# A graph layer on one core: two pieces of the edge list sorted side by side, and the order of the cold passes that follows from it

## The chip, the cores and the metric

The kernel runs on one core of a Trainium2 chip. The metric is device time in microseconds: before the change the median of three runs is 2072.53 us (2072.35 to 2072.87). The profile is one further execution of its own.

## The reference: what is computed

A layer over 6250 nodes of 256 features and 200000 edges, all in float32. The edges are sorted by `dst`, which is skewed towards low nodes; `src` is random.

```
xn = layernorm(x)
w  = sigmoid(relu(xn[dst] @ W1 + b1) @ W2 + b2)          # one weight per edge's far node
num, den = segment_sum(xn[dst] * w, src), segment_sum(w, src)
x  = x + where(den > 0, num / max(den, 1e-12), 0) + mix(xn)
x  = x + experts(layernorm(x))                          # 6 experts, the best 2 of them weighted
```

The part that matters here is the segment sum: for each of 200000 edges a row of the far node is added to the near node `src`. Six experts of three 256x256 layers are computed for every node.

## The kernel before, in words

**Rows.** Node by node a row `y = (xn * w, w)` is written to DRAM as three bfloat16 terms of 258 (`y_rows`, 774 values a row), by `node_rows`.

**Edges in pieces.** The kernel sorts the edges by `src` itself, in pieces of 65536 edges (128 partitions by 512). Two pieces are cold: `a` (edges 65536 on) and `c` (131072 on). The first 65536 edges are the hot piece `b`, whose `dst` are few: its edges are counted into small matrices instead of gathered. The last 3392 edges ("few", 27 tiles of 128) are gathered and scattered into a DRAM table one tile at a time (`few_edges`: a gather L519, a matmul L535, a copy `sm` by ACT, a scatter L540).

**The sort** (`sort`, L349) is a bitonic merge sort. Keys are made on DVE (`keys_of`), rows of 512 are sorted (`rows_sorted`, 9 levels), then seven levels merge over partitions (`merged`): turn the piece by four 128x128 transposes on PE and one copy by ACT (`turned`, L313 and L314), min/max steps, turn back, nine more min/max steps over the row. A step is two DVE instructions over 256 elements (L277 min, L278 max); the first step of a level negates one side (L262) and is two or four instructions. Each piece has its own tiles (`k_a`, `t_a` and so on) and its own chain of steps. When it is done, the sorted list is written to DRAM (L355).

**Order.** The order on each engine is written by hand: parts of the work are generators (`Line`), and `run` takes from a list of lines the first one that is due on a model clock; each step tells how much engine time it takes (`took` for a sort step) and how long its line then waits (`TURN` after a turn). First come a's sort, the node rows and the few edges' comparisons, with the sorts of c and b as filler behind them; `line_a2` is c's sort and `line_b` b's, and c stands ahead of b in the lists. Then the cold steps begin, one each 2200 ns of the model clock while the few edges last and one each 1300 ns after that, with the sorts, the head statistics (`head_squares`, `heads`) and a check for equal keys (`equal_keys`, which reads b's list back) between them.

**Cold steps** (`Cold`). For a block of two node tiles and a piece, the window of the sorted list that can hold its edges (12 tiles of 128 for each node tile) is loaded from DRAM by SP (L794), turned on PE (L818), copied by ACT (L820) and decoded on DVE (L827, L829, L868). Then for each tile of 128 edges: POOL gathers the rows of y by an indirect DMA (L880), DVE makes a one-hot matrix (L888), PE multiplies and sums (L905, three matmuls). Gathers are issued 10 steps ahead of the matmul (`AHEAD`), into 20 buffers (`GBUF`). `passes` (L836) lists what is done in which order: the first `LEAD` = 4 blocks take piece a alone, then the same 4 blocks take c alone, and from then on each block takes both. Sums of a alone are held as parts; there are `HELD` = 17 buffers for parts and sums. A window of c can be loaded only when c is sorted (`piece_sorted`, L919, which otherwise runs c's sort to its end on the spot).

**Main loop** (`Work`, L1349 on). Each cold step is followed by other work worth its share: node terms (L1102), hot sums of a block (one-hots L1049 and L1051, matmuls L1058 and L1077), and the experts (L1230, L1247). The hot sums of a block wait until the block's cold sums exist; the experts of a group of two blocks wait for its hot sums. The share leaves some 150 us (by the model) for the end.

The weights' loads on ACT's queue (L946 to L954) stand in the order behind the few edges; they go into memory that the few edges' tiles used.

Of the kernel before, what the change touches and what calls it, by code (L numbers as in the profile page):

```python
# [17 lines left out]
P = 128  # L18
# [6 lines left out]
LOW = 13  # L25
# [1 line left out]
HB = 8  # L27
GBUF = 20
AHEAD = 10
HELD = 17  # L30
LEAD = 4
LAST = 150000.0


# [15 lines left out]
def kernel(  # L50
# [45 lines left out]
    nc = tc.nc  # L96
# [64 lines left out]
    lists = {p.name: dram.tile([p.n + p.cap * P], FP, name=f"list_{p.name}") for p in pieces}  # L161
# [40 lines left out]
    sq_ps = sps.__enter__()  # L202
# [15 lines left out]
    def pool_of(p):  # L218
        return sp_small

    cnts = const.tile([P, len(pieces), NTHR], FP, name="cnts")
    raw = {}

    def raw_load(p):
        ends = []
        for nm, ap in (("src", src), ("dst", dst)):
            t = pool_of(p).tile([P, p.row], I32, name=f"{nm}_{p.name}")
# [6 lines left out]
    def keys_of(p):  # L234
        s_i, d_i = raw[p.name]
        pool = pool_of(p)
        key = pool.tile([P, p.row], I32, name=f"t_{p.name}", bufs=2)
        if p is hot:

            low = pool.tile([P, p.row], I32, name=f"k_{p.name}", bufs=2)  # L240
            nc.vector.tensor_scalar(low, s_i, BN - 1, None, op0=ALU.bitwise_and)
            nc.vector.scalar_tensor_tensor(low, d_i, 8, low, op0=ALU.logical_shift_left, op1=ALU.bitwise_or)
            nc.vector.tensor_scalar(key, s_i, 8, 18, op0=ALU.logical_shift_right, op1=ALU.logical_shift_left)
            nc.vector.tensor_tensor(key, key, low, op=ALU.bitwise_or)
        else:
            nc.vector.scalar_tensor_tensor(key, s_i, LOW, d_i, op0=ALU.logical_shift_left, op1=ALU.bitwise_or)
        k = pool.tile([P, p.row], FP, name=f"k_{p.name}", bufs=2)
# [32 lines left out]


    def took(n):
        return 2 * max(90.0, 60.0 + 1.05 * n)

    def rows_sorted(p, k):

        h = 1
        while h < p.row:
            g = h
            while g:  # L290
                o = pool_of(p).tile([P, p.row], FP, name=f"k_{p.name}", bufs=2)
                if g == h:
                    first(k, o, h, last=2 * h == p.row)
                else:
                    step(k, o, g)
                k, g = o, g // 2
                yield took(p.row // 2), 0
            h *= 2
        return k

    def turned(p, k, name, back):

        o = pool_of(p).tile([P, max(p.row, P)], FP, name=f"{name}_{p.name}", bufs=2)
        if p.row < P:
            ps = sq_ps.tile([P, 4 * P], FP, name="turn")
            a, b = (p.row, P) if back else (P, p.row)
            nc.tensor.transpose(ps[:b, :a], k[:a, :b], ident[:a, :a])
            nc.scalar.copy(o[:b, :a], ps[:b, :a])
            return o[:b, :a]
        for c0 in range(0, p.row, 4 * P):  # L310
# [3 lines left out]
            nc.scalar.copy(o[:, c0 : c0 + 4 * P], ps)  # L314
        return o

    def merged(p, k, m):

        t = turned(p, k, "t", False)
        yield 0, TURN  # L320
        g = h = 1 << (m - 1)
        while g:
            o = pool_of(p).tile([P, max(p.row, P)], FP, name=f"t_{p.name}", bufs=2)
            if p.row < P:
                o = o[: p.row, :P]
# [5 lines left out]
            yield took(p.row // 2 if p.row >= P else P // 2), 0  # L331
        k = turned(p, t, "k", True)
        yield 0, TURN
        g = p.row // 2
        while g:
            o = pool_of(p).tile([P, max(p.row, P)], FP, name=f"k_{p.name}", bufs=2)
            o = o[:, : p.row]
            step(k, o, g)
            k, g = o, g // 2
            yield took(p.row // 2), 0  # L340
        return k

    TURN = 2300.0


    pad = sp_small.tile([P, max(p.cap for p in pieces)], FP, name="pad")
    nc.vector.memset(pad.bitcast(I32), BASE | ((1 << LOW) - 1) << LOW)

    def sort(p):  # L349
        k = keys_of(p)  # L350
        yield 3.0 * p.row, 0
        k = yield from rows_sorted(p, k)
        for m in range(1, 8):
            k = yield from merged(p, k, m)
        nc.sync.dma_start(lists[p.name][: p.n].rearrange("(p t) -> p t", p=P), k)  # L355
        nc.sync.dma_start(lists[p.name][p.n :].rearrange("(p t) -> p t", p=P), pad[:, : p.cap])

    def counts(i):


        p = pieces[i]
        junk = pool_of(p).tile([P, p.row], BF, name=f"junk_{p.name}")
# [412 lines left out]
    with tc.manual_schedule(engines=ORDERED):  # L775
        clock[0] = 6000.0
        line_d.due = 12000.0
        line_l.due = 16000.0
        line_u[1].before = line_u[2].before = lines_y
        line_t.before = [line_l]  # L780
        line_u[0].due = 9000.0
        first_lines = [line_u[0], line_l, line_d] + lines_y + [line_a, line_t]
        while any(a.open for a in first_lines):
            run(first_lines + [line_q, line_h, line_u[1], line_a2, line_u[2], line_b], clock[0] + 1000.0)
        starts_of(0)


# [140 lines left out]
    known = [cold[0]]  # L928
    with tc.manual_schedule(engines=ORDERED):
        cold_edges = Cold(lambda p: p is cold[0] or piece_sorted(p))  # L930
        beside = [line_c, line_u[1], line_q, line_h, line_a2, line_u[2], line_b, line_e]
# [54 lines left out]


    line_w = Line(expert_loads())
    beside = [line_w, line_u[1], line_q, line_h, line_a2, line_u[2], line_b, line_e]
# [508 lines left out]
```

## Time and profile before

| what | us |
|---|---|
| median of three runs | 2072.53 |
| the profiled execution, its own time | 2076.93 |
| its span in the trace | 2075.1 |
| PE busy (85%) | 1761.2 |
| DVE busy (62%) | 1278.1 |
| POOL busy (58%), of it 1176 cold gathers 1133.0 | 1208.6 |
| ACT busy (28%) | 580.7 |
| first cold gather issued | 249.7 |
| lists written: a, c, b | 229.7, 420.8, 549.0 |
| first expert matmul (L1230) | 662.6 |
| last cold gather, last cold matmul | 1867.6, 1872.8 |

The page of the profile names engines by short names: PE is the matmul engine and PEld its weight load, DVE the vector engine, ACT the scalar engine, POOL the engine that issues the gathers, SP the one that issues most other DMAs. A row of the page's groups gives line, engine, operation, result and operands, how often, busy time and the mean in ns of one, and after the bar how long its engine had been idle and for whom. In a timeline a line begins with start and duration in us, and ends with the idle time before it and who ended that. In the table by stages each engine's busy time is followed by its count of instructions in brackets, and the row ends with the granted clock of PE, the share of the DMA engines and GB/s.

### The profile page before, as it was taken

What the parts mean: (1) busy time and instruction counts of PE and PEld (TensorE: products, weight loads), DVE (VectorE), ACT (ScalarE), POOL (GpSimd) and SP (SyncE); (2) the same over time, 40 slices, a digit from 0 to 9 for tenths busy, and PEclk for the clock granted to TensorE, in tenths of its full rate; (3) what the DMA queues carried; (4) which work ended last, traced back from release to release, by engine and by line L of the source; (5) the groups of instructions that cost most, each with busy time, mean ns of one, the idle gap of its engine ahead of it and who ended that gap; (6) DMA issues with size and microseconds to landing.
All of it is one profiled execution on the core that took longest, in us unless ns stands there. A gap on an engine that the chain in (4) does not pass through costs nothing.

```text
span 2075.1 us, 30397 instructions
## 1 busy us (share of the span) xinstructions
PE 1761.2 (85%) x9539; PEld 1175.5 (57%) x9539; DVE 1278.1 (62%) x5292; ACT 580.7 (28%) x1197; POOL 1208.6 (58%) x1243
## 2 busy tenths in 40 slices
PE   0564389635588999999999999999999999999997
PEld 0343277524355666666666666665666756566555
DVE  8799867948786555566565455555546565464322
ACT  6864464100011212222121221212212122222332
POOL 0000167877646777777777777777777777770000
PEclk9775589856689999999999999999999999999999
DMA  9562267567646566676666666666666566661000
GB/s 254 175 207 89 59 153 174 122 166 239 181 111 169 163 166 193 163 196 161 194 162 163 196 164 195 163 160 194 165 194 164 158 195 164 196 161 27 1 10 14
DMA packets 163586, 320.56 MB, mean 154 GB/s; under 512 B 31353, under 2 KB 104298, under 8 KB 163418
## 3 DMA queue, kind: packets, MB, share of 16 engines
q0 software_dynamic: 80800, 241.85, 44.1%
q1 hardware_dynamic: 77262, 76.15, 11.8%
q10 hardware_dynamic: 5356, 0.55, 0.3%
q8 instruction: 77, 1.26, 0.3%
q14 instruction: 91, 0.75, 0.1%
HBM read 285.06 MB, written 33.39 MB: 153 GB/s over the span
## 4 chain that ended last, share of the span: by engine, by line
PE 62%; DVE 8%; DMA 6%; issue 2%; POOL 1%; ACT 1%; SPq 0%; ACTq 0%; DVEq 0%; POOLq 0%
PE px L1230 23%; PE pu L905 15%; PE px L1247 11%; DMA gt<-y_rows,dsts 5%; PE ph L1077 5%; PE ph L1058 4%; DVE fr L1051 1%; PE px L1217 1%; DVE to L1049 1%; PE px L1137 1%; PE ph L1102 1%; DVE k_b L277 1%; DVE k_b L278 1%; POOL gt L880 1%; DVE hot L888 1%
## 5 line engine op out<-in xcount | busy, mean ns | idle before, releaser
L880 POOL DMA_INDIRECT gt<-y_rows,dsts x1176 | 1133.0, 963 | 634.9 <-DVE srcs L829 247.5
L905 PE MATMUL pu<-gt,hot 128*128 128x258 bf16 x3528 | 593.2, 285 | 28.6 <-DMA gt<-y_rows,dsts 27.4
L905 PEld LDWEIGHTS <-hot 128*128 128x128 bf16 x3528 | 355.4, 102 | 370.3 <-issue 292.8
L1239 ACT ACTIVATE h<-px,eb_t 128x512 f32<-128x512 f32 (+1 forms) x312 | 206.5, 662 | 477.4 <-PE px L1230 476.5
L1230 PE MATMUL px<-fT,ew_t 128*128 128x512 f32 (+1 forms) x624 | 303.9, 583 | 0.0
L1230 PE MATMUL px<-h,ew_t 128*128 128x512 f32 (+1 forms) x624 | 296.1, 569 | 0.0
L1247 PE MATMUL px<-ew_t,h 128*128 128x256 f32 (+1 forms) x1176 | 295.3, 379 | 0.0
L888 DVE TENSOR_SCALAR hot<-count,loc 128x128 bf16<-128x128 bf16 x1176 | 271.1, 271 | 20.6 <-PE pu L905 20.1
L1256 DVE SCALAR_TENSOR_TENSOR acc<-px,gate,acc 128x256 f32<-128x256 f32 (+1 forms) x294 | 128.7, 478 | 219.4 <-PE px L1247 219.0
L1051 DVE TENSOR_SCALAR fr<-count,rdl 128x128 bf16<-128x128 bf16 x884 | 226.6, 271 | 40.7 <-PE ph L1058 40.1
L1247 PEld LDWEIGHTS px<-ew_t,h 128*128 128x128 f32 (+1 forms) x1176 | 204.0, 190 | 25.8 <-issue 4.8
L1058 PE MATMUL ph<-to,fr 128*128 128x256 bf16 x884 | 183.7, 284 | 21.0 <-DVE fr L1051 15.6
L1049 DVE TENSOR_SCALAR to<-count,hloc 128x256 bf16<-128x256 bf16 x612 | 183.7, 302 | 7.4 <-PE ph L1058 7.2
L1060 ACT CAST cn<-ph 128x256 bf16<-128x256 f32 x150 | 54.5, 372 | 299.0 <-PE ph L1058 298.4
L1077 PE MATMUL ph<-yh,cn 128*128 128x258 bf16 x882 | 129.3, 274 | 0.8 <-ACT cn L1060 0.7
L1058 PEld LDWEIGHTS <-fr 128*128 128x128 bf16 x884 | 87.7, 99 | 63.8 <-DVE fr L1051 42.1
L1087 DVE TENSOR_TENSOR cs<-ph,cs 128x258 f32<-128x258 f32 x49 | 20.9, 427 | 152.4 <-PE ph L1077 151.2
L1230 PEld LDWEIGHTS px<-fT,ew_t 128*128 128x128 f32 x624 | 98.4, 195 | 23.4 <-issue 16.5
L1230 PEld LDWEIGHTS px<-h,ew_t 128*128 128x128 f32 x624 | 96.0, 190 | 22.6 <-issue 18.2
L1077 PEld LDWEIGHTS <-cn 128*128 128x128 bf16 x882 | 86.0, 98 | 18.4 <-issue 5.2
L563 PE MATMUL turn<-ident,xs 128*128 128x128 f32 (+1 forms) x98 | 27.5, 402 | 78.1 <-ACT xs L554 73.1
L563 PEld LDWEIGHTS turn<-ident,xs 128*128 128x128 f32 (+1 forms) x98 | 16.9, 194 | 88.4 <-issue 50.1
(242 smaller groups left out, 1767.1 us busy)
## 6 DMA issues: line engine op xcount, KB each, us to landing
gt<-y_rows,dsts POOLq DMA_INDIRECT x1176
xs<-in_x_dram SPq DMA_DIRECT2D x24, 512.0 KB
y_rows<-ys SPq DMA_DIRECT2D x10, 774.0 KB
table<-zero SPq DMA_DIRECT2D x50, 129.0 KB
tb<-table SPq DMA_DIRECT2D x49, 129.0 KB
xnT_d<-xnT SPq DMA_DIRECT2D x12, 512.0 KB
xt<-xnT_d SPq DMA_DIRECT2D x12, 512.0 KB
u<-in_x_dram SPq DMA_DIRECT2D x12, 512.0 KB
```

The lines of the kernel that those rows point to most:

```text
L880: nc.gpsimd.indirect_dma_start(out=gt.rearrange("p k w -> p (k w)"), out_offset=None, in_=y_rows, in_offset=bass.IndirectOffsetOnAxis(ap=d ...
L888: nc.vector.tensor_scalar(hot1, count[:, half * P : (half + 1) * P], loc[:, j : j + 1], None, op0=ALU.is_equal)
L905: nc.tensor.matmul(self.pu, hot1, gt[:, k], start=(start and k == 0), stop=(stop and k == TERMS - 1))
L1049: nc.vector.tensor_scalar(made[j1], count, loc[:, j1 : j1 + 1], None, op0=ALU.is_equal)
L1051: nc.vector.tensor_scalar(fr, count[:, :P], rdl[:, d1, j1 : j1 + 1], None, op0=ALU.is_equal)
L1058: nc.tensor.matmul(pa, matrices[i], made[j], start=(j == j0), stop=(j == j1 - 1))
L1060: nc.scalar.copy(cn[:, d], pa)
L1077: nc.tensor.matmul(pu[:, :W], cn[:, d, s * P : (s + 1) * P], yh[:, d, k], start=(d == 0 and k == 0), stop=(d == HOT - 1 and k == TERMS - 1),)
L1230: nc.tensor.matmul(ph[:, :rows], w[:, e, c, f * P : (f + 1) * P], ins[:, c, :rows], start=(c == 0), stop=(c == CB - 1),)
L1239: nc.scalar.activation(h[:, f, :rows], ph[:, :rows], AF.Relu, bias=bc)
L1247: nc.tensor.matmul(po[:r, j - j0], h2[:, c, j * P : j * P + r], ew_t[2][:, e, c, :], start=(c == 0), stop=(c == CB - 1),)
L1256: nc.vector.scalar_tensor_tensor(acc[:r, j, :], po[:r, j - j0], gate[:r, j, e : e + 1], acc[:r, j, :], op0=ALU.mult, op1=ALU.add)
```

## The change

Pieces c and b are sorted by one chain: their keys stand in the two halves of tiles of 1024 (`k_cb`, `t_cb`), each min/max instruction covers 512 elements instead of 256 (the first steps 256 instead of 128), a turn is eight transposes and two copies, and both lists are written when the one sort ends. There is one line for it, `line_b`, in the place of `line_a2` and `line_b`; a is sorted as before. `LEAD` is 6 instead of 4, so six blocks (144 gathers) take a alone, then the same six take c alone. `HELD` is 18. The model's price of a sort step is 150 + 1.05 n ns an instruction instead of 60 + 1.05 n (at least 90). The pace of the cold steps no longer slips when a step overruns it (`due += 2200.0` for `due = max(due + 2200.0, clock[0])`, and so for 1300). c's counts and starts are asked for by `piece_sorted(cold[1])` at the latest when both lines are through.

```diff
-HELD = 17
-LEAD = 4
+HELD = 18
+LEAD = 6
...
+    ROW = 512
+    def keys_of(ps, name):
+        key = sp_small.tile([P, len(ps) * ROW], I32, name=f"t_{name}", bufs=2)
+        for i, p in enumerate(ps):
+            s_i, d_i = raw[p.name]
+            part = key[:, i * ROW : (i + 1) * ROW]
...
     def took(n):
-        return 2 * max(90.0, 60.0 + 1.05 * n)
+        return 2 * (TT0 + 1.05 * n)
-    def rows_sorted(p, k):
+    def rows_sorted(k, name, width):
         h = 1
-        while h < p.row:
+        while h < ROW:
...
-                o = pool_of(p).tile([P, p.row], FP, name=f"k_{p.name}", bufs=2)
+                o = sp_small.tile([P, width], FP, name=f"k_{name}", bufs=2)
...
-                yield took(p.row // 2), 0
+                yield took(width // 2), 0
...
+    TT0 = 150.0
...
-    def sort(p):
-        k = keys_of(p)
-        yield 3.0 * p.row, 0
-        k = yield from rows_sorted(p, k)
+    def sort(ps):
+        name, width = "".join(p.name for p in ps), len(ps) * ROW
+        k = keys_of(ps, name)
+        yield 3.0 * width, 0
+        k = yield from rows_sorted(k, name, width)
         for m in range(1, 8):
-            k = yield from merged(p, k, m)
-        nc.sync.dma_start(lists[p.name][: p.n].rearrange("(p t) -> p t", p=P), k)
-        nc.sync.dma_start(lists[p.name][p.n :].rearrange("(p t) -> p t", p=P), pad[:, : p.cap])
+            k = yield from merged(k, name, width, m)
+        for i, p in enumerate(ps):
+            nc.sync.dma_start(lists[p.name][: p.n].rearrange("(p t) -> p t", p=P), k[:, i * ROW : (i + 1) * ROW])
+            nc.sync.dma_start(lists[p.name][p.n :].rearrange("(p t) -> p t", p=P), pad[:, : p.cap])
...
-    line_a, line_a2, line_b = (Line(sort(p)) for p in pieces)
+    line_a, line_b = Line(sort(pieces[:1])), Line(sort(pieces[1:]))
...
-        while line_a2.open or line_u[1].open:
-            run([line_u[1], line_a2], clock[0] + 1000.0)
+        while line_b.open or line_u[1].open:
+            run([line_u[1], line_b], clock[0] + 1000.0)
...
-            due = max(due + 2200.0, clock[0])
+            due += 2200.0
...
-            due = max(due + 1300.0, clock[0])
+            due += 1300.0
             run(beside, due)
+        piece_sorted(cold[1])
```

More of the change, by code (lines that the diff above doesn't have):

```diff
@@ L216 @@
     nc.vector.tensor_scalar(odd, even, SIGN, None, op0=ALU.bitwise_xor)
-    def pool_of(p):
-        return sp_small
     cnts = const.tile([P, len(pieces), NTHR], FP, name="cnts")
@@ L226, in raw_load @@
         for nm, ap in (("src", src), ("dst", dst)):
-            t = pool_of(p).tile([P, p.row], I32, name=f"{nm}_{p.name}")
+            t = sp_small.tile([P, p.row], I32, name=f"{nm}_{p.name}")
             nc.sync.dma_start(t, ap[p.start : p.start + p.n].rearrange("(p t) -> p t", p=P))
@@ L232 @@
     raw_load(cold[0])
[L234 to L247, printed above, removed]
+    ROW = 512
[4 more added lines that the diff above has]
+            part = key[:, i * ROW : (i + 1) * ROW]
+            if p is hot:
+                low = sp_small.tile([P, len(ps) * ROW], I32, name=f"k_{name}", bufs=2)[:, :ROW]
+                nc.vector.tensor_scalar(low, s_i, BN - 1, None, op0=ALU.bitwise_and)
+                nc.vector.scalar_tensor_tensor(low, d_i, 8, low, op0=ALU.logical_shift_left, op1=ALU.bitwise_or)
+                nc.vector.tensor_scalar(part, s_i, 8, 18, op0=ALU.logical_shift_right, op1=ALU.logical_shift_left)
+                nc.vector.tensor_tensor(part, part, low, op=ALU.bitwise_or)
+            else:
+                nc.vector.scalar_tensor_tensor(part, s_i, LOW, d_i, op0=ALU.logical_shift_left, op1=ALU.bitwise_or)
+        k = sp_small.tile([P, len(ps) * ROW], FP, name=f"k_{name}", bufs=2)
         ki = k.bitcast(I32).rearrange("p (t two) -> p t two", two=2)
@@ L282, in took @@
     def took(n):
-        return 2 * max(90.0, 60.0 + 1.05 * n)
-    def rows_sorted(p, k):
+        return 2 * (TT0 + 1.05 * n)
+    def rows_sorted(k, name, width):
         h = 1
-        while h < p.row:
+        while h < ROW:
             g = h
             while g:
-                o = pool_of(p).tile([P, p.row], FP, name=f"k_{p.name}", bufs=2)
+                o = sp_small.tile([P, width], FP, name=f"k_{name}", bufs=2)
                 if g == h:
-                    first(k, o, h, last=2 * h == p.row)
+                    first(k, o, h, last=2 * h == ROW)
                 else:
@@ L296, in rows_sorted, with turned @@
                 k, g = o, g // 2
-                yield took(p.row // 2), 0
+                yield took(width // 2), 0
             h *= 2
         return k
[L301 to L310, printed above, removed]
+    def turned(k, name, width):
+        o = sp_small.tile([P, width], FP, name=name, bufs=2)
+        for c0 in range(0, width, 4 * P):
             ps = sq_ps.tile([P, 4 * P], FP, name="turn")
@@ L315, in turned, with merged @@
         return o
-    def merged(p, k, m):
-        t = turned(p, k, "t", False)
+    def merged(k, name, width, m):
+        t = turned(k, f"t_{name}", width)
         yield 0, TURN
@@ L322, in merged @@
         while g:
-            o = pool_of(p).tile([P, max(p.row, P)], FP, name=f"t_{p.name}", bufs=2)
-            if p.row < P:
-                o = o[: p.row, :P]
+            o = sp_small.tile([P, width], FP, name=f"t_{name}", bufs=2)
             if g == h:
@@ L330, in merged @@
             t, g = o, g // 2
-            yield took(p.row // 2 if p.row >= P else P // 2), 0
-        k = turned(p, t, "k", True)
+            yield took(width // 2), 0
+        k = turned(t, f"k_{name}", width)
         yield 0, TURN
-        g = p.row // 2
+        g = ROW // 2
         while g:
-            o = pool_of(p).tile([P, max(p.row, P)], FP, name=f"k_{p.name}", bufs=2)
-            o = o[:, : p.row]
+            o = sp_small.tile([P, width], FP, name=f"k_{name}", bufs=2)
             step(k, o, g)
             k, g = o, g // 2
-            yield took(p.row // 2), 0
+            yield took(width // 2), 0
         return k
+    TT0 = 150.0
     TURN = 2300.0
@@ L347 @@
     nc.vector.memset(pad.bitcast(I32), BASE | ((1 << LOW) - 1) << LOW)
-    def sort(p):
-        k = keys_of(p)
-        yield 3.0 * p.row, 0
-        k = yield from rows_sorted(p, k)
+    def sort(ps):
[3 more added lines that the diff above has]
+        k = yield from rows_sorted(k, name, width)
         for m in range(1, 8):
-            k = yield from merged(p, k, m)
-        nc.sync.dma_start(lists[p.name][: p.n].rearrange("(p t) -> p t", p=P), k)
-        nc.sync.dma_start(lists[p.name][p.n :].rearrange("(p t) -> p t", p=P), pad[:, : p.cap])
+            k = yield from merged(k, name, width, m)
+        for i, p in enumerate(ps):
+            nc.sync.dma_start(lists[p.name][: p.n].rearrange("(p t) -> p t", p=P), k[:, i * ROW : (i + 1) * ROW])
+            nc.sync.dma_start(lists[p.name][p.n :].rearrange("(p t) -> p t", p=P), pad[:, : p.cap])
     def counts(i):
         p = pieces[i]
-        junk = pool_of(p).tile([P, p.row], BF, name=f"junk_{p.name}")
+        junk = sp_small.tile([P, p.row], BF, name=f"junk_{p.name}")
         for b in range(SB - 1 if p is hot else 0, NTHR, SB if p is hot else 1):
@@ L783 @@
         while any(a.open for a in first_lines):
-            run(first_lines + [line_q, line_h, line_u[1], line_a2, line_u[2], line_b], clock[0] + 1000.0)
+            run(first_lines + [line_q, line_h, line_u[1], line_u[2], line_b], clock[0] + 1000.0)
         starts_of(0)
@@ L930 @@
         cold_edges = Cold(lambda p: p is cold[0] or piece_sorted(p))
-        beside = [line_c, line_u[1], line_q, line_h, line_a2, line_u[2], line_b, line_e]
+        beside = [line_c, line_u[1], line_q, line_h, line_u[2], line_b, line_e]
         run(beside[1:], clock[0] + 9000.0)
@@ L988 @@
     line_w = Line(expert_loads())
-    beside = [line_w, line_u[1], line_q, line_h, line_a2, line_u[2], line_b, line_e]
+    beside = [line_w, line_u[1], line_q, line_h, line_u[2], line_b, line_e]
     with tc.manual_schedule(engines=ORDERED):
```

## The prediction

> **What bounds the kernel now.** I read the slices of the page first, then busy time by stages, then the timeline of POOL, and last the timeline of DVE and ACT around the sort.
>
> ```profile
> PE   0564389635588999999999999999999999999997
> DVE  8799867948786555566565455555546565464322
> POOL 0000167877646777777777777777777777770000
> PEclk9775589856689999999999999999999999999999
> ```
>
> Each digit is a fortieth of the span (52 us). PE is full only from slice 13 on; before that it has idle time and a low granted clock. POOL starts at 250 us, stands at 7 (never 9), dips at slice 11 and stops at 1868.
>
> ```profile
> 0.00:249.50 249.50, 102.30 (x362) 65.85 (x363) 215.10 (x674) 152.72 (x327) 1.62 (x12) 0.72 0.53 158
> 249.50:454.00 204.50, 148.22 (x983) 119.33 (x981) 155.13 (x500) 73.49 (x187) 155.43 (x135) 0.81 0.62 146
> 454.00:549.00 95.00, 53.33 (x273) 38.09 (x273) 72.97 (x251) 8.70 (x18) 73.18 (x74) 0.65 0.72 212
> 549.00:662.50 113.50, 82.41 (x489) 51.40 (x490) 85.00 (x430) 14.38 (x39) 64.27 (x67) 0.80 0.52 144
> 662.50:1873.10 1210.60, 1188.23 (x6703) 783.52 (x6701) 688.05 (x3216) 271.74 (x518) 914.06 (x957) 0.99 0.64 175
> 1873.10:2075.10 202.00, 186.72 (x736) 117.35 (x734) 61.87 (x226) 59.68 (x110) 0.00 (x0) 0.96 0.04 11
> ```
>
> Busy PE, PEld, DVE, ACT, POOL with counts. I cut at events: first gather (249.5), last scatter of the few edges (454), end of the last sort (549), first expert matmul L1230 (662.5), last cold matmul L905 (1873.1). What limits the middle is seen one gather at a time:
>
> ```profile
> 1210.97 0.95 POOL L880 DMA_INDIRECT gt<-y_rows,dsts  x1 [0.30 <-issue]
> 1212.23 0.96 POOL L880 DMA_INDIRECT gt<-y_rows,dsts  x1 [0.30 <-issue]
> 1213.49 0.95 POOL L880 DMA_INDIRECT gt<-y_rows,dsts  x1 [0.30 <-issue]
> ```
>
> 0.95 us plus a fixed 0.30: POOL is saturated although the slices say 7. From 662.5 to 1867.6 it issues 957 gathers, 1.26 us each, and after 664 never waits longer than 0.31. At 662.5 it has issued 81 + 72 + 67 = 220 and PE has used 200, the whole 20 buffers of lead; the lead drains, and PE idles 22 us in that stage (21 of them after 1100). So **POOL's row of 1176 gathers bounds the kernel**, PE almost as tight; the end is last gather + 5.5 + 202. POOL loses time in one place: 549 to 662.5, 67 gathers where 90 fit.
>
> The sort ends late for a reason that is not DVE:
>
> ```profile
> 453.99 1.49 POOL L540 DMA_INDIRECT table<-sm,few_row  x1 [0.30 <-issue]
> 457.51 0.42 ACTq L946 DMA_DIRECT2D rw_t<-in_L_ffn_router_w_dram  x1
> 459.17 0.59 ACT L314 COPY t_b<-turn 128x512 f32<-128x512 f32 x1 [28.04 <-DMA eb_t<-in_L_ffn_expert_b_dram]
> 459.79 0.90 DVE L262 SCALAR_TENSOR_TENSOR t_b<-t_b 128x128 f32<-128x128 f32 x4 [20.71 <-ACT t_b L314]
> ```
>
> (POOL, ACT and DVE of one timeline.) The weight loads on ACT's queue reuse memory that the last scatter still reads; ACT is held 28 us, the sort's copy stands behind them, DVE idles 20.7. POOL sets this moment.
>
> **The change, part by part.** Counts and places come from the order of both programs' instructions.
>
> *Price of a step.* Rows of DVE:
>
> ```profile
> L277 DVE TENSOR_TENSOR k_b<-k_b 128x256 f32<-128x256 f32 x99 | 41.6, 421 | 12.1 <-ACT k_b L314 10.8
> L262 DVE SCALAR_TENSOR_TENSOR k_c<-k_c 128x256 f32<-128x256 f32 x2 | 0.8, 422 | 0.0
> L760 DVE TENSOR_TENSOR xt<-xt 128x512 f32<-128x512 f32 x1 | 0.7, 691 | 7.7 <-DMA wt_a<-list_c 7.7
> 432.63 0.25 DVE L888 TENSOR_SCALAR hot<-count,loc 128x128 bf16<-128x128 bf16 x1
> 432.80 0.42 DVE L277 TENSOR_TENSOR k_b<-k_b 128x256 f32<-128x256 f32 x1
> 433.13 0.42 DVE L278 TENSOR_TENSOR k_b<-k_b 128x256 f32<-128x256 f32 x1
> 433.58 0.42 DVE L277 TENSOR_TENSOR k_b<-k_b 128x256 f32<-128x256 f32 x1
> ```
>
> A min/max pair starts every 0.78 us (0.39 a step, they overlap), a one-hot takes 0.17. Doubling the width adds 691 - 421 = 0.27: a joint step is 0.66, a pair 1.32 where two pairs were 1.56. A joint first step is about 0.36 (four of 128x128 take 0.90). Bounds for the joint pair: 1.1 (each 0.27 + 0.27, overlap hiding all the rest) to 1.56 (no saving). I take 1.32, from the nearest row. Over 120 pairs the sort sheds some 30 us of DVE; the question is what waits for it.
>
> *To the first gather.* Ahead of the end of a's sort stood 63 steps of c (3 for keys 1.4, 28 firsts 6.3, 32 steps 12.5: 20 us); now 45 joint ones (7 for keys 4.2, 20 firsts 7.2, 18 steps 11.9: 23), and the few edges' last comparison comes before it (1 us). DVE is 215 of 249 busy here, so it is paid: 249.7 becomes 253.2 (bounds 247 to 257). After a: 34 steps (13 us) against 20 (13 us).
>
> *To the last scatter.* POOL's order has 74 cold gathers ahead of scatter 27, not 81: 7 x 1.255 = 8.8 less. DVE sheds about 36 us here (322 steps become 140), all beside POOL. 253.2 + 204.3 - 8.8 = **448.7**. POOL's only stalls (scatters waiting 3.7, 3.0, 2.0 for ACT) are kept.
>
> *To the end of the joint sort.* DVE resumed 5.8 after the scatter; a turn now has eight transposes and a second ACT copy, +0.59: 455.1. Left then are 94 steps (before: 172): 8 firsts 2.9, 43 pairs 56.8, 50 one-hots 8.3, decodes 2.0, and five turns. A turn left DVE idle some 1.2; four more transposes (1.1) and fewer one-hots in the gap make it 2.7: 13.5. Sum 83.5, **538.6** where c and hot ended at 420 and 549.
>
> *POOL runs dry.* This is new. No gather of c can come before 538.6, so a alone feeds POOL: six blocks, 144 gathers. The last 32 sort steps are forced in one go ahead of one-hot 123, when a's last pass asks for c's first window. With 20 buffers POOL gets to gather 133 at 448.7 + 1.8 + 59 x 1.27 = 525.4; PE comes free of the last turn 18 steps (12 us) before the end, 526.6; ten more gathers last to 539.3. Number 144 stands behind c's window: list written (549.02 to 552.78 before, 3.8), two window loads (0.9 + 1.9), transpose, copy, decode: 8 us, so POOL resumes at **546.6** with 143 issued, 7 us lost. Before had 152 by then.
>
> *To the first expert matmul.* Hot sums need c's parts now: block 0 only at cold matmul 168, then one block every 24 (30.2 us). A block's burst took 14.3 us (563.26 to 577.55), so DVE (14 + 24 x 0.17 + 6 of sums) has room, and POOL's lead of up to 20 gathers rides over it: the loss of 23 gathers goes. But the first L1230 stands at cold 248, not 200: 546.6 + 97 x 1.26 + 3.5 = 672.3 for cold 240, a burst and 3 more: **689.5**, 27 later.
>
> *To the end.* PE's order from there holds the same work but 48 gathers' matmuls less (976 to 928; 0.50 each, 24 us): 1188 - 24 = 1164 busy. POOL: 256 issued, 920 x 1.26 + 5.5 = 1165. Both equal; I add 5 for their catching on each other: 1170, where 1210.6 were. The tail is identical in both orders: 202. Four more DVE adds L913 (0.42) and two more decodes hide under POOL; at 2 us in all if not. HELD adds one buffer of 18, never the limit here.
>
> Sum: 689.5 + 1170 + 202 = 2061.5 against the span 2075.1, **13.6 less**. The profiled execution took 2076.93, the median is 2072.53, 2.6 below the span; so **2059**.
>
> **Rivals.**
> - *POOL starves longer; slower.* Every microsecond by which c's first window comes after 546.6 is paid in full: break-even at 560. It comes so if the wide step saves nothing (43 x 0.24 = 10) and turns expose all their transposes (another 10): +20, **2079**. For it: POOL has nothing else to issue. Against: 691 ns is measured.
> - *PE can't fill the last stage.* If its 22 us of idle stay, 1164 + 22: 2077.5, **2075**. For: 1164 against 1165 leaves no slack. Against: those idles came after the lead was used up.
> - *POOL's first stage tightens too; more gain.* To the last scatter I kept 195.5 us, but POOL's own work there is 101 x 1.255 + 27 x 1.98 = 180. If DVE's lighter load ends the stalls and the long gathers (15) and the first gather stays at 249.7 (3.5), all that follows moves up by 19: **2040**. For it: 36 us of DVE gone from that stage. Against: those stalls come at its start, from scatters that wait for ACT.
> - *Wider steps slow POOL.* Gathers take 1.03 us beside the sort (83.11 us for 81) and 0.955 later. If a gather waits for the step it meets, the extra 0.07 grows by 691/421 to 0.12: 190 POOL operations x 0.046 = 9, **2068**. The Trainium skill, GPSIMD Engine Reference, section 1 Specifications, says that POOL's SBUF interfaces are shared with VectorE and that instructions with two SBUF inputs contend; the slower gathers agree. It speaks against the change only by length, since the wide steps are fewer.
>
> **How the numbers follow.** Forecast 0.52, starving 0.18, PE 0.14, tight first stage 0.10, slower POOL 0.06. A difference under 0.2% (4 us) can't be told here from none. Faster: 0.50 + 0.10 + 0.03 = 0.63; same: 0.02 + 0.11 + 0.02 = 0.15; slower: 0.18 + 0.03 + 0.01 = 0.22. The range runs from the tight first stage to the starving case, 2040 to 2080.
>
> **What would show it.** First gather near 253, last scatter near 449, joint steps of 690 ns, list_c written near 539, a gap in POOL around gather 144 ending near 547 and no gaps of over 1 us from there to 690, first expert matmul near 690, last cold matmul near 1860, 202 after. It is wrong if list_c is written after 552, or if POOL waits for buffers again between 547 and 690, or if PE idles over 15 us after that.

## The result, and the profile after

The changed kernel takes 2066.50 us, the median of 7 runs (2062.76 to 2070.45), against 2072.18 us for the kernel before in 7 runs on the same chip (2068.03 to 2072.87): a ratio of 0.9974, 95% interval 0.9962 to 0.9987. It is faster, by 5.7 us, where 13.6 were forecast. On two of the four chips used further below every kernel takes some 14% longer, so for the experiments ratios to the kernel before on the same chip are compared, and not times. Line numbers have shifted a little: the cold gather is L877 now (L880 before), the cold matmul L902 (L905), min and max L278 and L279 (L277 and L278), a turn's copy L309 (L314), the first expert matmul L1228 (L1230), the list's write L352 (L355).

The slices of the page after:

```profile
PE   0474279746468899999999999999999999999997
DVE  8689966657657765565646555564655666464322
POOL 0000077877777777777777777777777777760000
PEclk9666579956678999999999999999999999999999
```

POOL's dip (the 4 in the twelfth slice before) is gone: it stands at 7 or 8 from its first full slice on. But its fifth slice is empty, where a 1 stood, and DVE has 6 and 8 in its second and third slices where it had 7 and 9: something in the first 250 us became slower. Three rows of the busy times by stages, cut at the same events as before (up to the first gather; from the joint list to the first expert matmul; from there to the last cold matmul):

```profile
0.00:263.20 263.20, 102.41 (x362) 62.69 (x363) 216.34 (x643) 158.89 (x351) 1.62 (x12) 0.70 0.50 150
...
541.40:699.30 157.90, 117.16 (x709) 74.82 (x710) 100.60 (x514) 15.44 (x44) 119.51 (x127) 0.80 0.67 186
699.30:1861.60 1162.30, 1159.23 (x6557) 767.32 (x6556) 685.40 (x3173) 270.42 (x513) 871.63 (x916) 1.00 0.64 176
```

The first stage is 13.7 us longer than before (263.2 to 249.5). In the third row PE is busy 1159.2 of 1162.3 us: it idles 3.1 us where it idled 22. POOL's last gather is at 1848.7 and the last cold matmul at 1861.4, 12.7 us behind, where it was 5.2. So PE, and no longer POOL, looks like the bound of this stage; a run below shows it for the kernel with six blocks alone, by taking work off PE.

| event, us | before | forecast | after |
|---|---|---|---|
| a's list issued | 229.7 | | 245.0 |
| first gather | 249.7 | 253.2 | 263.3 |
| last scatter of the few edges | 454.0 | 448.7 | 455.7 |
| joint list issued (before: c, b) | 420.8, 549.0 | 538.6 | 541.4 |
| gather 144 | | 546.6 | 551.85 |
| first expert matmul | 662.6 | 689.5 | 699.3 |
| last cold matmul | 1872.8 | 1859.5 | 1861.4 |
| end of the span | 2075.1 | 2061.5 | 2063.8 |
| the execution's own time | 2076.93 | | 2065.69 |

POOL around the end of the joint sort:

```profile
540.53 1.02 POOL L877 DMA_INDIRECT gt<-y_rows,dsts  x1 [0.30 <-issue]
541.86 0.94 POOL L877 DMA_INDIRECT gt<-y_rows,dsts  x1 [0.30 <-issue]
...
550.60 0.95 POOL L877 DMA_INDIRECT gt<-y_rows,dsts  x1 [0.30 <-DVE hot L885]
551.85 0.95 POOL L877 DMA_INDIRECT gt<-y_rows,dsts  x1 [0.30 <-PE pu L902]
```

No gap: the dry spell that was forecast for 539.3 to 546.6 did not come. The joint sort's steps (a row of the groups) and ACT's copy that it resumes with after the last scatter (issued at 455.69):

```profile
L278 DVE TENSOR_TENSOR k_cb<-k_cb 128x512 f32<-128x512 f32 x99 | 67.4, 680 | 13.8 <-ACT k_cb L309 13.0
```
```profile
460.85 1.07 ACT L309 COPY t_cb<-turn 128x512 f32<-128x512 f32 x2 [17.77 <-DMA eb_t<-in_L_ffn_expert_b_dram]
```

A joint step takes 680 ns where 691 was assumed, and a pair starts every 1.32 to 1.33 us (1.32 assumed). The hold of ACT behind the last scatter is there as before: ACT has waited 17.8 us, and the copy starts 5.2 us after the scatter.

What delays the first gather is seen in ACT's first turn of a, in whom DVE waits for up to the issue of a's list, and in the sums of busy time up to there. The kernel before (the turn, DVE's waits up to 229 us: us in total, times, longest; the sum up to 229.6):

```profile
95.35 0.56 ACT L314 COPY t_a<-turn 128x512 f32<-128x512 f32 x1
```
```profile
DVE yh L600 <- ACT w L586: 9.1, 1, 9.1
DVE ys L600 <- ACT w L586: 2.4, 2, 1.4
DVE k_a L277 <- ACT k_a L314: 0.9, 1, 0.9
```
```profile
sum 229.60, PE 90.42 PEld 58.73 DVE 201.47 ACT 141.78 POOL 1.62; mean PE 18.08 PEld 11.75 DVE 40.30 ACT 28.36 POOL 0.32
```

The kernel after (the waits up to 244 us, the sum up to 244.7):

```profile
113.93 0.59 ACT L309 COPY t_a<-turn 128x512 f32<-128x512 f32 x1 [2.03 <-PE turn L308]
```
```profile
DVE yh L597 <- ACT w L583: 10.3, 1, 10.3
DVE ys L597 <- ACT w L583: 6.0, 4, 3.6
DVE t_a L263 <- ACT t_a L309: 5.1, 3, 2.7
DVE yh L605 <- ACT yh L603: 2.8, 1, 2.8
```
```profile
sum 244.70, PE 90.69 PEld 55.72 DVE 205.17 ACT 149.10 POOL 1.62; mean PE 18.14 PEld 11.14 DVE 41.03 ACT 29.82 POOL 0.32
```

The first turn of a, with which the seven merge levels start, is 18.6 us later. In the order of DVE's instructions 171 others stand ahead of the first step behind that turn, not 162, with 4 joint steps more. The nine more are instructions of the node rows (L595 to L605), which have come in front of a's steps. Some of them wait for ACT, and a's chain waits behind them. Up to the end of a's sort DVE is busy 205.2 us (before 201.5) and idle 39.5 (before 28.1). So 3.7 us of the delay are more work and 11.4 are idle time. By all rows of the two lists of waits, some 7 us of the idle time are waits of the node rows for ACT (20.5 us, before 13.8), and some 5 are waits of a's sort for its own turns (5.8 us, before 0.9).

**Theory.** The model's new price of a sort step (`TT0`) makes `run` take a's steps less densely in the first stage; the late first gather that follows is paid to the end, and hides the joint sort's end. The gain comes from six blocks, which close POOL's lull. **Rivals**: the joint steps put in front of a's sort delay it; or an earlier first gather would only open the dry spell; or it is the joint sort that gains.

### The profile page after: what moved, and what is told of

It reads as the page before. It is cut to its first block, busy times and chain, and to the rows that moved or that the text cites. A ratio compares the mean times of both kernels' runs of the same rounds, so it can differ in the third digit from the quotient of the medians.

```text
span 2063.8 us, 30158 instructions
## 1 busy us (share of the span) xinstructions
PE 1756.6 (85%) x9541; PEld 1171.1 (57%) x9541; DVE 1256.2 (61%) x5000; ACT 577.4 (28%) x1199; POOL 1213.7 (59%) x1243
## 4 chain that ended last, share of the span: by engine, by line
PE 68%; DVE 4%; DMA 3%; issue 1%; ACT 1%; POOL 0%; SPq 0%; DVEq 0%; POOLq 0%; ACTq 0%
PE px L1228 25%; PE pu L902 16%; PE px L1245 12%; PE ph L1075 5%; PE ph L1056 4%; DMA gt<-y_rows,dsts 3%; PE px L1215 1%; PE px L1135 1%; PE ph L1100 1%; DVE to L1047 1%; DVE fr L1049 1%; PE px L1128 0%; PE px L1141 0%; PE pT L815 0%; PE turn L308 0%
## 5 line engine op out<-in xcount | busy, mean ns | idle before, releaser
L877 POOL DMA_INDIRECT gt<-y_rows,dsts x1176 | 1136.3, 966 | 618.9 <-DVE srcs L826 261.1
L902 PE MATMUL pu<-gt,hot 128*128 128x258 bf16 x3528 | 598.8, 285 | 48.1 <-DMA gt<-y_rows,dsts 38.3
L902 PEld LDWEIGHTS <-hot 128*128 128x128 bf16 x3528 | 354.7, 102 | 395.7 <-issue 305.6
L1228 PE MATMUL px<-fT,ew_t 128*128 128x512 f32 (+1 forms) x624 | 301.4, 578 | 0.0
L1228 PE MATMUL px<-h,ew_t 128*128 128x512 f32 (+1 forms) x624 | 296.3, 569 | 0.0
L1228 PEld LDWEIGHTS px<-fT,ew_t 128*128 128x128 f32 x624 | 97.2, 193 | 23.3 <-issue 16.6
L1228 PEld LDWEIGHTS px<-h,ew_t 128*128 128x128 f32 x624 | 95.9, 190 | 22.9 <-issue 18.5
L817 ACT COPY keys<-pT 128x25 f32<-128x25 f32 (+2 forms) x56 | 10.5, 187 | 251.3 <-PE pT L815 250.0
```

What stands on the lines that cost most here:

```text
L877: nc.gpsimd.indirect_dma_start(out=gt.rearrange("p k w -> p (k w)"), out_offset=None, in_=y_rows, in_offset=bass.IndirectOffsetOnAxis(ap=d ...
L902: nc.tensor.matmul(self.pu, hot1, gt[:, k], start=(start and k == 0), stop=(stop and k == TERMS - 1))
L1228: nc.tensor.matmul(ph[:, :rows], w[:, e, c, f * P : (f + 1) * P], ins[:, c, :rows], start=(c == 0), stop=(c == CB - 1),)
```

## The experiments

The experiments are four groups of four kernels, each group on a chip of its own. Only ratios to the kernel before are compared between groups; each group ran that kernel too. It took 2348.14 and 2371.90 us on the chips of the first two groups and 2076.48 and 2074.08 us on those of the last two.

### The price of a step: old price in the changed kernel

```diff
     def took(n):
-        return 2 * (TT0 + 1.05 * n)
+        return 2 * max(90.0, 60.0 + 1.05 * n)
```

> The changed kernel with the model's old price of a sort step (at least 90, 60 + 1.05 n ns an instruction), all else as changed. In the order of DVE the same 45 joint steps stand ahead of the end of a's sort, but 162 other instructions ahead of a's first turn in place of 171. Theory A, the new price spread a's steps so that DVE waits for ACT in the first stage, and the 13.6 us by which the first gather came later are paid at the end: first gather 250 to 254, time 2054 to 2058. Rival B, the wide joint steps in front of a's sort delay it: first gather 260 or later, time 2064 to 2068. Rival C, an earlier first gather only opens the gap ahead of gather 144 that the prediction spoke of: first gather 252, a gap of some 8 us in POOL near 545, time 2061 to 2065.

Ratio 0.9949 (0.9925 to 0.9973) on a slower chip, first gather 252.3. Again, with the changed kernel beside it on the other slower chip:

> The changed kernel once more, unaltered, so that the experiments have it beside them on their own chip and there is a second trace of it. On the first chip it was 0.9974 of the kernel before, with its first gather at 263.3 us and the list of the joint sort issued at 541.4. If the late first gather lies in the order that the planner chose, it is again between 262 and 267, and the ratio to before 0.995 to 1.000. If the 263.3 was a chance of one execution (the profile before had 249.7), the first gather comes near 253. On a chip with a lower granted clock PE is the bound of the last stage in both kernels; then the gain of POOL's shorter row counts less and the ratio is 0.998 to 1.004.

> The changed kernel with the planner's old price of a sort step, once more, now with the changed kernel beside it on the same chip. If the new price is what puts the first gather at 263, and that delay is paid at the end, this one is 8 to 12 us (0.4 to 0.5%) faster than the changed kernel, with its first gather at 250 to 254. If POOL or PE takes the delay up again before the end, the two are within 0.2% of each other, although the first gathers differ by 11 us.

The changed kernel 1.0024 (0.9999 to 1.0049), first gather 267.6; with the old price 0.9961 (0.9937 to 0.9985), first gather 254.5. The ratios lie 0.0063 apart, some 15 us, more than the 8 to 12 expected. And on a chip as fast as that of the result:

> The changed kernel a third time, as the bar for the two beside it. First gather between 262 and 269. Ratio to before 0.995 to 0.999 on a chip whose PE is granted its full clock in the last stage (0.9974 on the first), 1.000 to 1.005 on a slow one (1.0024 on the second).

> The changed kernel with the old price of a sort step once more. On slow chips it was 0.995 and 0.996 of before, 0.0064 below the changed kernel. If the delay of the first gather is paid whole on a chip with the full clock too, the ratio is 0.990 to 0.993, 10 to 13 us below the changed kernel. The rival: there PE is full in the last stage (3.1 us idle in the trace after), an earlier POOL only meets a full PE, and less than half of it, under 6 us, is left: 0.9945 to 0.9975.

The changed kernel 0.9962 (0.9949 to 0.9975), first gather 263.6; with the old price **0.9904** (0.9888 to 0.9919), first gather 254.2: 13.2 us of median for 9.4 us of first gather in the two traces. The rival that a full PE swallows the earlier start is refuted. With the old price ACT's first turn of a is at 98.05, where it is 113.93 in after and 95.35 in before. The spans of these two traces differ by 18.2 us: 9.4 from the first gather, 3.9 from the last stage (1162.6 and 1166.5), 3.3 from the tail (199.0 and 202.3), 1.6 from the rest; the first is the order's, the others vary between executions too.

### The price alone in the kernel before, and the joint steps in front of a

The price edit in the kernel before, which has no joint step:

```diff
-        return 2 * max(90.0, 60.0 + 1.05 * n)
+        return 2 * (150.0 + 1.05 * n)
```

> The kernel before with the new price of a sort step alone (150 + 1.05 n ns), pieces sorted one after the other and four blocks of a. Theory A: first gather 258 to 264 in place of 249.7, though no step is wide; the cold steps then stand denser beside the sort (first expert matmul at cold step 216, not 200), which wins some of it back: time 2068 to 2078. Rival B: first gather 247 to 253, time 2062 to 2070.

Ratio 1.0072 (1.0044 to 1.0099), more than the 0.3% at most that was expected; first gather 264.4, with the first turn as late as after:

```profile
116.18 0.59 ACT L314 COPY t_a<-turn 128x512 f32<-128x512 f32 x1 [1.69 <-PE turn L313]
```

The changed kernel without the joint sort as filler in the first lines, which leaves 23 joint steps ahead of the first decode where there were 65:

```diff
-            run(first_lines + [line_q, line_h, line_u[1], line_u[2], line_b], clock[0] + 1000.0)
+            run(first_lines + [line_q, line_h, line_u[1], line_u[2]], clock[0] + 1000.0)
```

> The changed kernel with the joint sort left out of the lines that run beside a's sort: 23 joint steps stand ahead of the first decode in place of 65, so some 27 us of DVE work move behind the first gather. Theory A (order by price) and B (wide steps in the way) both expect the first gather 15 to 27 us earlier, 236 to 248. They part at the end: by B the whole kernel follows, 2050 to 2058. By A together with the dry spell of the prediction the joint sort ends no earlier, near 545, POOL has used up a's 144 gathers by 525 and waits some 25 us for c's first window: 2062 to 2070.

Ratio 1.0159 (1.0123 to 1.0195), first gather 266.8. Both theories had expected the first gather at 236 to 248, and both missed. The 23 joint steps that are left ran at 22 to 43 us, in front of a's first turn, so this edit does not clear the way of a's sort altogether. And where the filler is gone DVE stands idle: up to the end of a's sort it is busy 191.7 us, 13.4 less than in the changed kernel, but idle 56.6, 17.0 more. The rival of the joint steps is refuted by the price alone, which made the first gather late without one of them, and by the run under the next heading, which has 43 of them in front and an early first gather. This kernel was slow for another reason: its joint list came at 592.1, and POOL stood dry for 34.7 and then 6.6 us.

### Which price

The old price for steps of 256, the new one for the joint steps of 512:

```diff
-        return 2 * (TT0 + 1.05 * n)
+        return 2 * ((60.0 if n <= 256 else TT0) + 1.05 * n)
```

> The changed kernel with the old price for steps of up to 256 and the new one for the joint steps of 512. The order that it gives has a's sort ended behind 43 joint steps and as many other DVE instructions as with the old price. If the first gather is late because the narrow steps of a are priced at 450 to 700 ns each (their rows: 421), it is back at 251 to 255 here and the ratio is that of the old price, 0.989 to 0.992 on the full clock. If the price of the joint steps does it, the first gather stays at 262 to 267 and the ratio at 0.995 to 0.998.

Ratio 0.9940 (0.9926 to 0.9955), first gather **249.2**. So it is the price of a's narrow steps that made it late. But the ratio is not the 0.989 to 0.992 that was expected with it: it is only 0.002 to 0.003 below the changed kernel's (0.9974 and 0.9962), some 5 to 7 us, where the old price throughout gave 13.2. POOL at the end of the joint sort, whose list this kernel issued at 536.0:

```profile
537.57 0.94 POOL L877 DMA_INDIRECT gt<-y_rows,dsts  x1 [0.81 <-PE pu L902]
544.61 0.99 POOL L877 DMA_INDIRECT gt<-y_rows,dsts  x1 [6.09 <-DVE hot L885]
```

This is the forecast dry spell, at its place and nearly its size: POOL idle 6.1 us (7 forecast), gather 144 at 544.6, 8.6 us after the list (8.0 forecast). The rival "an earlier first gather only opens the dry spell" is right for this kernel and not for the one with the old price throughout: there the joint steps too are cheap to the model, so they are taken earlier, and the list is issued at 518.9. So the new price costs twice: some 5 to 7 us through a's steps, which make the first gather late, and, by the difference of 0.9940 and 0.9904, some 7 through the joint steps, which make their list late.

### Four blocks with the joint sort

```diff
-HELD = 18
-LEAD = 6
+HELD = 17
+LEAD = 4
```

> The changed kernel with four blocks that take their first piece alone, as before, and the sorts still side by side. My theory of the dry spell: until the joint sort ends, POOL has only 96 gathers of these blocks to issue instead of 144. At 1.25 to 1.28 us each from 263 on, with the 27 scatters of the few edges between (some 2 us each), these 96 are issued by about 440 us, so POOL has nothing left for about 100 us, and gather 97 comes some 10 us after the list of the joint sort (which may come 5 to 10 earlier, with fewer one-hots ahead of it). The 39 gathers that the changed kernel issues in that time, 50 us, are lost: slower than the changed kernel by 35 to 50 us, a ratio to before of 1.013 to 1.022. The rival: the lead of six hides nothing that PE does not hide anyway, and this runs within 0.3% of the changed kernel.

Ratio 1.0284 (1.0249 to 1.0318): 61 us slower than the changed kernel on that chip, more than the 35 to 50 expected. The trace shows the prediction's rival of a starving POOL in full, in two gaps around the list's issue at 543.3:

```profile
532.13 1.33 POOL L877 DMA_INDIRECT gt<-y_rows,dsts  x1 [52.98 <-PE pu L902]
...
552.70 0.99 POOL L877 DMA_INDIRECT gt<-y_rows,dsts  x1 [7.00 <-DVE hot L885]
```

60 us in all. On that chip, a slower one, the changed kernel itself had gaps of 11.3 and 6.2 us at this place (its list came at 573.1 there).

### Everything but the joint sort, and six blocks alone

Everything of the change but the joint sort (six blocks, 18 buffers, new price, new pace; c and b sorted one after the other):

```diff
-    line_a, line_b = Line(sort(pieces[:1])), Line(sort(pieces[1:]))
+    line_a, line_a2, line_b = (Line(sort(p)) for p in pieces)
```

> The changed kernel in all but the sort side by side: six blocks of a alone, 18 held sums, new price, steady pace, but c and then b sorted one after the other. First expert matmul at cold step 248 as in the changed kernel; b's list later, near 580. Theory P, the gain comes from keeping POOL without a gap, which six blocks and the pace do: no gap in POOL, time 2062 to 2070. Rival S, the wide steps are needed: b's list and with it the hot sums come too late, POOL waits for held sums, time 2074 to 2090.

Ratio 1.0052 (1.0023 to 1.0081), on the first group's chip; first gather 264.2, as late as with the price alone. That lies where rival S put it and not theory P. But b's list came at 646.1, far behind the 580 expected, POOL's longest gap was 6.1 us, and the interval overlaps that of the changed kernel on the other slower chip (0.9999 to 1.0049). So this run does not decide what the joint sort is worth beside the new price. Then the kernel before with six blocks and nothing else, with a second trace of before beside it:

```diff
-HELD = 17
-LEAD = 4
+HELD = 18
+LEAD = 6
```

> The kernel before, unaltered, for a second trace of it beside the others of this call. Its first gather was at 249.7 us and its last sort ended at 549.0 on the first chip. If these are set by the planner's order they come again within 3 us and 10 us; the ratio to itself is 1.000 within 0.3%. On a slow chip the last stage is longer, with a granted clock below 1 and POOL waiting for PE; on one like the first, the stage from the first expert matmul to the last cold matmul takes about 1210 us, POOL waiting for nothing.

> The kernel before with six blocks that take their first piece alone, not four, and one buffer more for held results; the sorts one after the other and the price as before. This is that part of the change alone. From the difference of the two runs with the new price on the before order (1.0072 with four blocks, 1.0052 with six) it should bring 0.1 to 0.3%: ratio 0.997 to 0.999. If the sorts side by side carry the gain, it is within 0.1% of before; if the gain is all in the six blocks, it equals the changed kernel with the old price, 0.995 or below. POOL has 144 gathers before the second piece is needed, so the lull after the sort (67 gathers where 90 fit, in before) should go from the trace.

> The kernel before with six blocks that take their first piece alone and the separate sorts, once more, as the bar for the three beside it. On the third chip it was 0.9895 of before, with its first gather at 250.6, its first expert matmul at 688.0, and 1164.7 us from there to the last cold matmul. Again 0.988 to 0.991 on a chip with the full clock; on a slow one 0.992 to 1.000.

The kernel before against itself 1.0002 (0.9989 to 1.0015). Six blocks alone **0.9895** (0.9881 to 0.9909) and, in the next group, 0.9897 (0.9883 to 0.9911). That is 22.2 and 20.6 us, as much as the changed kernel with the old price (0.9904). I had expected 0.1 to 0.3%, worked out from runs on a slower chip that carried the new price; that was wrong. The stages from the end of b's sort to the first expert matmul, and from there to the last cold matmul, of this kernel and of the changed one with the old price (joint list to first expert, and on):

```profile
548.20:688.00 139.80, 104.08 (x636) 66.83 (x637) 95.73 (x487) 14.86 (x42) 105.96 (x112) 0.82 0.66 179
688.00:1852.70 1164.70, 1160.94 (x6556) 767.34 (x6555) 686.70 (x3173) 270.55 (x513) 871.91 (x915) 1.00 0.64 175
```
```profile
518.90:690.10 171.20, 122.72 (x708) 75.84 (x709) 101.09 (x514) 15.40 (x44) 129.78 (x137) 0.77 0.66 181
690.10:1852.70 1162.60, 1159.28 (x6555) 766.78 (x6554) 685.85 (x3173) 270.21 (x513) 870.67 (x916) 1.00 0.64 176
```

POOL issues 112 gathers in 139.8 us, one each 1.25: the lull (67 in 113.5 before) is gone. From the first gather to the first expert matmul it is 437.4 us with the sorts apart and 435.9 with the joint sort; DVE is busy 1286 us in the one and 1256 in the other. The joint sort takes 30 us off DVE, and the first expert matmul came no earlier for it. The joint sort alone, with four blocks and the old price, was not run.

### Five blocks

```diff
-HELD = 17
-LEAD = 4
+HELD = 18
+LEAD = 5
```

> The kernel before with five blocks that take their first piece alone, separate sorts. The hot sums and with them the first expert matmul start one block earlier (cold matmul 224, not 248), so the lull in POOL that four blocks have can come back in part. If the gain is the lull's alone and 120 gathers reach past the sort's end as far as needed, it equals six blocks (0.988 to 0.991 on the full clock). If it goes with the number of blocks, it is half of the gain: 0.993 to 0.996.

Ratio 0.9904 (0.9890 to 0.9919): as good as six. The first expert matmul is at 665.2 and the last stage takes 1183.0 us with 937 gathers; the last cold matmul is 5.8 us behind the last gather, so POOL bounds it here. Between the end of b's sort and the first expert matmul POOL issues 88 gathers in 118.5 us, one each 1.35, with one gap of 3.8 us left: most of the lull is closed. So the gain goes with the closed lull and not with the number of blocks.

### What bounds the last stage

In the changed kernel, and in the kernel with six blocks and separate sorts, only two of three cold matmuls are kept, so the third bf16 term of every cold sum is left out.

```diff
-            for k in range(TERMS):
+            for k in range(2):
...
-                    self.pu, hot1, gt[:, k], start=(start and k == 0), stop=(stop and k == TERMS - 1)
+                    self.pu, hot1, gt[:, k], start=(start and k == 0), stop=(stop and k == 1)
```

> The changed kernel with two of the three bf16 terms of each gathered row multiplied; it leaves the third (smallest) term of every cold sum out, with one matmul of three for each of 1060 gathers, some 0.1 to 0.13 us of PE each. If PE bounds the stage from the first expert matmul on (PE idled 3.1 us there in the trace after), that stage shortens until POOL's gathers bound it: the last cold matmul then stands some 5 us behind the last gather instead of 12.7, the last gather itself comes no earlier than POOL's pace of 1.25 us allows, and the total falls by 8 to 20 us (0.4 to 1%) on the first chip's clock and by more (up to 100 us, some 4%) where the clock is low and PE is far behind. If POOL alone is the bound, the last gather stays where it is and the total falls by less than 4 us.

> The same kernel (six blocks, separate sorts) with two of the three bf16 terms of each gathered row multiplied; it leaves the third term of every cold sum out. In the kernels with six blocks the last stage took 1162 to 1167 us whatever stood ahead of it, with PE busy but for some 3 us. If PE's own work bounds it, that work shrinks by about 930 x 0.12 = 110 us there and the stage falls to POOL's pace, about 915 x 1.255 + 6 = 1154 us: the total is 8 to 15 us below the kernel above, and the last cold matmul stands 5 to 7 us behind the last gather, not 14. If POOL's gathers bound it (PE's busy time being what the gathers let it do), nothing changes within 3 us.

In the kernel with six blocks and separate sorts: 2045.71 beside 2053.49 us, 7.8 less, and the last cold matmul 5.0 us behind the last gather (18.2 in the kernel beside it). The stage:

```profile
685.20:1841.10 1155.90, 1092.94 (x5628) 681.99 (x5627) 684.95 (x3173) 269.11 (x513) 873.04 (x916) 0.98 0.64 177
```

1155.9 us where 1163.6 were, with 67 us of PE work less (I had expected 110 less, and 1154). PE now waits 53.3 us for gathers in this stage, 2.4 at the longest; in the kernel beside it it waits for none. So with six blocks PE bounds the last stage, and POOL's row lies only some 8 us below it. On a slower chip the same edit in the changed kernel gave 0.9984 beside 1.0024, 10 to 12 us, far from the 100 that I had allowed there. In the changed kernel's last stage on that chip neither PE nor POOL is full (some 178 and 127 us busy of 200), and what limits it stayed open.

## Why the prediction was wrong, point by point

- **To the first gather: the step of the mechanism that failed.** It forecast 3.5 us later, it was 13.6. The step counted DVE's instructions ahead of the end of a's sort and charged their busy time, and that was right: 3.7 us. It took the idle time for constant, and put the new price at nothing. The new price moved node-row instructions that wait for ACT in front of a's steps, and idle DVE grew by 11.4 us, some 7 of them in these waits and some 5 in waits of a's sort for its own turns. The old price took the delay away (252.3, 254.5, 254.2), the price alone brought it (264.4). I read the price as part of the model, not as an edit of the schedule. In the median the new price costs 13.2 us; with the old one the gain is 21.5 us in the third group, more than forecast. Of the 13.2 the late first gather alone, taken back at 249.2, was worth only 5 to 7, because the dry spell then opened; the rest is the late list.
- **From span to median: the term that put the total out.** The forecast put the median 2.6 below the span; after, it is 2.7 above. That is 5.3 of the 7.5 us between 2059 and 2066.5. The 2.6 came from one profiled execution: that of before (2076.93) lay 4.7 above the median of its 7 runs, that of after 0.8 below. The spans differ by 11.3 us, the medians by 5.7; 5.6 are this. In another group the kernel before ran from 2073.46 to 2080.19 in 8 executions: one span is good to some 4 us, and a forecast of 13.6 needed that said.
- **To the last scatter**: 192.4 us from the first gather, 195.5 forecast. The third rival had half of its mechanism: the stalls of 3.7, 3.0 and 2.0 us are gone, and POOL waits no longer than 0.31 there. But the longer gathers of the fourth rival are there too: 74 of them took 79.53 us, 1.07 each, where 81 took 83.11, 1.03 each. With the scatters and the few edges' gathers that is some 5.5 us more. So the stage came out 3.1 us shorter than forecast, and not 15 as the third rival had it. In the next stage 61 gathers take 1.07 us each where they took 0.99, another 5. So the 9 us of the fourth rival stand in POOL's busy time. How much of them was paid no run shows: with shorter gathers POOL would have used up a's 144 sooner and then waited for c's first window.
- **To the end of the joint sort**: 85.7 us after the last scatter, 89.9 forecast. Step, pair and hold came as priced; which of its other terms was 4.2 us too long no run separates.
- **The dry spell** of 7 us did not come, because POOL was later and had some 10 us of gathers left when the list came. With the first gather at 249.2 it came, 6.1 us.
- **To the first expert matmul**: 147.5 us from gather 144, 142.9 forecast; no gap and no wait for buffers, as forecast. POOL had issued 262 gathers by then and not 256, so PE stood further behind it.
- **The last stage**: 1162.3, 1170 forecast. PE busy is 1159 (1164 forecast), and the 5 us for PE and POOL catching on each other, which no run had shown, were not needed. The rival "PE can't fill the last stage" is refuted: 3.1 us idle.
- **The span** missed by 2.3 us only, and that is luck: the first expert matmul came 10 us late, as the first gather had, and the last stage was 8 us shorter than forecast.
- **What the change is made of**, from the third group: six blocks bring 22.2 us; with the joint sort and the new pace added, at the old price, the time is 0.7 us higher, which is nothing; the new price costs 13.2; together 8.3 less than before. The new pace by itself was not tried. The version with six blocks alone is faster than both kernels of this study, and so is the changed one with the old price.

## What to carry to other kernels

A price in a scheduler's model is an edit of the order on every engine that it schedules: diff the order of the first stage for what now stands ahead of the chain that releases the bound engine, and look for instructions there that wait for another engine, since their idle time counts and not their busy time. A truer price need not give a better order: the new price is nearer to the measured pairs (838 for 780 ns, and 1375 for 1325, where the old gave 658 and 1195) and cost 13 us. And before a saving on one engine is counted, ask what waits for it; here 30 us of DVE, with the new pace, were worth nothing that shows, and moving 48 gathers of a in front of c's first was worth some 20 us.

## What the runs showed of the hardware

The same program took 2348 and 2372 us on two chips and 2072 to 2076 on others, with one core at work. In the last stage the granted clock was 1.00 in the changed kernel on the chip of the result, and from 0.89 to 0.97 on one of the slower chips in stretches of 200 us, with PE busy some 178 of 200. With matmuls taken out the granted clock was lower: a mean of 0.858 for 0.877 over the profiled executions there, and 0.98 for 1.00 in the last stage on the fourth group's chip. The Trainium skill, TensorE: Matmul & The Clock Gate, Part 1, describes a gate that falls back when PE idles, and this lower clock beside a less busy PE agrees with it in direction; the longest wait of PE in that last stage is 2.4 us, and how long a wait the gate needs no run here shows. What made the two chips slower no run here shows.

A gather takes 1.02 us beside joint min and max steps and 0.94 once the last of them has ended (540.53 and 541.86 in the fence above; the last step ends at 541.3). The Trainium skill, GPSIMD Engine Reference, section 1 Specifications, says that POOL shares its SBUF interfaces with VectorE and contends with instructions that have two SBUF inputs; the 0.08 us agree with it. The rule is not all of it: in the kernel before, ten of the twelve gathers that start from 534 to 549 us, among narrow steps that have two inputs too, took 0.94 to 0.96 us. No run here separates the width of a step from the rest.
